# A graph network on one core: the first rows picked ahead of the rest, and the bias adds moved into layer 1's pairs

## The chip, the cores and the metric

The kernel runs on one core of a Trainium2 chip. The metric is the device time of one execution in microseconds. TensorE (PE in the profile, PEld for its weight loads), VectorE (DVE), ScalarE (ACT), GpSimd (POOL) and SyncE (SP) each work through a queue of their own in order and wait for each other by semaphores.

## The reference

Three edge-convolution layers over a graph of 2500 nodes and 80000 edges (sorted by `dst`), 256 features each. With h0 = relu(layernorm(x)):

```python
def _edge_conv(x, src, dst, W, b):
    xi = x[dst]
    xj = x[src]
    m = jnp.concatenate([xi, xj - xi], axis=-1) @ W + b
    s = jax.ops.segment_sum(m, dst, num_segments=N)
    cnt = jax.ops.segment_sum(jnp.ones((dst.shape[0],), m.dtype), dst, num_segments=N)
    return s / jnp.maximum(cnt, 1.0)[:, None]
...
for W, b in ((W0, b0), (W1, b1), (W2, b2)):
    h = jax.nn.relu(_edge_conv(h, src, dst, W, b))
    xs.append(h)
cat = jnp.concatenate(xs, axis=-1)
return cat @ Wf + bf
```

The result is x plus this. The message of an edge is linear in its two nodes, so a layer is h times (upper half of W minus lower half), plus the matrix A of edge counts between nodes times (h times the lower half), divided by the node's count of edges.

## The kernel before

The nodes are 20 tiles of 128 rows; `acc` holds one row of 256 numbers for each and gathers the result. The kernel has four parts.

**The head** (about the first 60 us) does three things at once, on all engines: it normalizes x and turns it (`hT`), it multiplies the tiles by the lower half of W0 (`pz`, split into a high and a low part, `zh` and `zl`) and by the first quarter of Wf, and it builds the first fifth of A. For A, the destinations are cut into windows of 6 nodes, 417 windows in four blocks of 128. To find where the edges of a window begin, `first` takes the first destination of each of 128 rows of `dst_i`; a product with a shifted identity on PE (`find_next`) puts the next row's first destination beside it; `find_rows` makes `behind` and `pick`, matrices of 128 x 512 (four blocks of 128 windows) which mark for every window the row that holds its limit; a product with `pick` fetches that row (`pick_half`, "pk"), ScalarE counts in it (`count_half`, "sg"), `search` ("se") works out a start, and POOL gathers 256 edges for every window (`get_edges`, "ge"). From the edges come keys, and from these, on DVE, `one_m` and `one_n` (`compare`, "B"), matrices of zeros and ones whose products on PE (`counts`, "C") are the counts of A.

The order of the head is written out by hand: `order` (L916) is a string of names with a number each, `perform` calls them one by one, and as nearly every engine call goes through `InOrder`, every engine's queue keeps that order. `st` are the statistics of two tiles, `rs`, `sq`, `sc` the steps to the scale and offset of a group of tiles, `N` their normalization (on DVE for tile 0, on ScalarE for tiles 1 to 3, on POOL from tile 4 on), `T` and `R` turning and taking what was turned, `Z` and `F` the products with W0 and Wf, `warm` a number of empty products of 128 x 512 put before the next product that asks for a bank of PSUM. "warm8" stands ahead of the product of `find_next`, "warm7" ahead of the first product with `pick`.

The x tiles come in five loads (`chunks`, L431). The third is on ScalarE's queue behind the load of `dst_i`, the others on SP's, where the loads of W0 and Wf stand between them. `small_numbers` ("io") turns three integer ramps into bfloat16 and float32.

**Layer 0** goes over five groups of destinations (504 columns, the last 486): PE multiplies zh and zl by the block of A (`a`), while the next block is built between the products and written to memory. In its last group, side work (`first_forms`) prepares layer 1: weights and the first two pairs of tiles are split into parts, and then four adds put the final bias `bf` on all 20 tiles of `acc`, 5 tiles (128 x 1280) each.

**Layers 1 and 2** begin with a node stage: for each of ten pairs of tiles (`Nodes`), DVE and ScalarE split `hT` (`Split`, into `staged`), PE multiplies by W and Wf (12 products), ScalarE and DVE take them into `zf`, `zh`, `zl`, `acc` and the sums `sh` and `sl`, and between these PE works off the last group of A alone (8 products for each pair of tiles). Then come the pairs: groups 0 and 1, then 2 and 3 of A, five chunks of four tiles each. A chunk takes seven products of combined blocks ("b11", "b21", "b22", "r1" to "r4") instead of eight. `Stream` (L1307) makes the blocks five steps ahead of PE: ScalarE copies b11, b21 and b22 into `block`; DVE adds in place for r1 and r2 (`staged` from `staged`), which ScalarE then copies; DVE writes r3 and r4 straight into `block`. The add of r2 writes over b22, so it waits until ScalarE has copied that.

**The end** multiplies layer 2's result by the last quarter of Wf and writes `acc` out.

Of the kernel before, what the change touches and what calls it, by code (L numbers as in the profile page):

```python
# [11 lines left out]
OP = mybir.AluOpType  # L12
# [301 lines left out]
def by_windows(ctx: ExitStack, tc: tile.TileContext, x, src, dst, Ws, bs, Wf, bf, out, missing):  # L314
    nc = tc.nc
    PE, DVE, ACT, POOL, SP = nc.tensor, nc.vector, nc.scalar, nc.gpsimd, nc.sync
    PEo, DVEo, POOLo, ACTo, SPo = (InOrder(tc, e) for e in (PE, DVE, POOL, ACT, SP))
    P = 128
    N, D = x.shape
    E = src.shape[0]  # L320
    NT = (N + P - 1) // P
# [5 lines left out]
    W = 6  # L327
    CH = 2
    S = 8
# [4 lines left out]
    WG = (NW + P - 1) // P  # L334
    IN_LAST = NW - (WG - 1) * P
    NB = NT * W
    N1 = NT * KEEP
# [52 lines left out]
    iota_m = const.tile([P, P], BF16, name="iota_m")  # L390
    iota_n = const.tile([P, NB], BF16, name="iota_n")
    deg = const.tile([P, WG, W], F32, name="deg")
    gsum = const.tile([P, WG, W + 2], F32, name="gsum")
    nc_ = const.tile([P, W + 2], F32, name="nc_")
    deg_b = const.tile([P, WG, W], BF16, name="deg_b")
    lim = const.tile([P, WG], F32, name="lim")
# [29 lines left out]
    def load_x(queue, a, b):  # L426
        queue.dma_start(acc[:, a:min(b, NT - 1), :], xr[:, a:min(b, NT - 1), :])
        if b == NT:
            queue.dma_start(acc[:LAST, NT - 1, :], x[(NT - 1) * P:N, :])

    chunks = [(0, 2), (2, 6), (6, 12), (12, 16), (16, NT)]  # L431
    load_x(SPo, *chunks[0])
    load_x(SPo, *chunks[1])
    load_x(ACTo, *chunks[2])
# [6 lines left out]
    def new_raw(l):  # L441
        raws[l] = raw_pools[-1].tile([P, DC, 2, D], F32, name="wbf", bufs=1)

    def load_wb(l, queue=SP):
        new_raw(l)
        ws[l] = (wts[l] if l == 1 else wpool.tile([P, DC, D], F32, name="wt")), raws[l][:, :, 0, :]
        queue.dma_start(ws[l][1], Ws[l][D:2 * D, :].rearrange("(c p) d -> p c d", p=P))
# [6 lines left out]
    def load_wf(l, queue=SP):  # L454
        if l == L:
            new_raw(l)
        wfs[l] = raws[l][:, :, 1, :]
        queue.dma_start(wfs[l], Wf[l * D:(l + 1) * D, :].rearrange("(c p) d -> p c d", p=P))

    load_wb(0, SPo)  # L460
    load_x(SPo, *chunks[3])
    load_wf(0, SPo)
    load_x(SPo, *chunks[4])
# [12 lines left out]
    im_i = pp.tile([P, NT * S], I32, name="im_i")  # L476
# [3 lines left out]
    nc_i = pp.tile([P, W + 2], I32, name="nc_i")  # L480
# [30 lines left out]
    limr = pp.tile([P, WG * P], F32, name="limr")  # L511
    first = pp.tile([P, 1], F32, name="first")
    after = pp.tile([P, 1], F32, name="after")
    behind = pp.tile([P, WG * P], F32, name="behind")
    pick = pp.tile([P, WG * P], F32R, name="pick")
# [8 lines left out]


    def small_numbers():
        DVEo.tensor_copy(iota_m, im_i[:, :P])
        DVEo.tensor_copy(iota_n.rearrange("p (c t) -> p t c", c=W), im_i.rearrange("p (t c) -> p t c", c=S)[:, :, 1:W + 1])
        DVEo.tensor_copy(nc_, nc_i)

    def limits():
        DVEo.tensor_copy(lim, lim_i)
# [16 lines left out]

    def find_rows():  # L550
        DVEo.tensor_add(after, ahead[0][:, 0:1], after)
        DVEo.tensor_scalar(behind, limr, after, None, op0=OP.is_gt)
        DVEo.scalar_tensor_tensor(pick, limr, first, behind, op0=OP.is_gt, op1=OP.subtract)

    row = pp.tile([P, WG], F32, name="row")

# [2 lines left out]
    def pick_half(i, o):  # L559
        pr = picked[i, o] = warmed(bank())  # L560
        PEo.matmul(pr[:, :HR], pick[:, i * P:(i + 1) * P], dst_r[:, o * HR:(o + 1) * HR], start=True, stop=True)

    def count_half(i, o):

        pr = picked.pop((i, o))
        junk = pp.tile([P, HR], BF16, name="junk1")
        ACTo.activation(junk, pr[:, :HR], AF.Sign, bias=unlim[:, i:i + 1], accum_out=base[:, o, i:i + 1])
        if o == 0:
            ACTo.copy(row[:, i:i + 1], pr[:, 0:1])
# [291 lines left out]
    def layer(l, g, a, own, PE=PE, ACT=ACT):  # L861
# [38 lines left out]
    a = new_a(0)  # L900
    acts = {
        "lim": limits, "first": find_first, "next": find_next, "pick": find_rows,
        "dstr": lambda: ACTo.copy(dst_r[:, MORE:], dst_i),
        "pk": lambda i: pick_half(i // 10, i % 10), "sg": lambda i: count_half(i // 10, i % 10),
        "se": lambda i: search(*((0, 1), (1, WG))[i]), "ge": get_edges,
        "aw": find_away, "ka": key_parts, "km": key_low, "kb": key_high, "kt": key_turn,
        "k1": lambda i: key_copy(i, 0), "k2": lambda i: key_copy(i, 1),
        "io": small_numbers, "ws": lambda: DVEo.tensor_sub(ws[0][0], ws[0][0], ws[0][1]),
        "st": stats, "rs": lambda g: spread(*groups[g]), "sq": lambda g: roots(*groups[g]),
        "sc": lambda g: scales(*groups[g]), "N": normalize, "T": turn, "R": take_turned,  # L910
# [3 lines left out]
        "warm": keep_warm,  # L914
    }
    order = """  # L916
        warm8 lim io first next dstr st0 rs0 sq0 pick sc0 warm7 N0 pk00 sg00 pk01 st1 T0 pk11 R0 sg01 st2 rs1 sq1 Z0 pk30 se0
        sg11 sc1 pk20 N1 st4 st5 sg30 ge0 T1 st6 R1 F0 sg20 pk21 st7 pk10 H0 F1 rs3 st3 sq3 sc3 G0 st9
        L0 sg21 N6 pk31 aw0 ka0 kb0 Z1 N5 st8 N7 G1 T6 rs4 sg10 sg31 km0 T5 se1 kt0 R6 H1 F6 sq4 sc4 k10 k20
        rs2 Z6 ge1 L1 T7 B0 R5 R7 Z5 B1 C0 B2 aw1 ka1 G6 H6 N9 H5 C1 T9 F7 E0 ge2 kb1 R9 sq2 km1 E1 kt1 C2 B3 k21 Z9  # L920
        k11 N8 L6 B4 sc2 aw2 E2 L5 C3 B5 C4 T8 E3 E4 C5 V9 ka2 ge3 kb2 R8 E5 H9 aw3 km2 Z7 N2 N3 C6 ka3 kb3 H7 F8 G7 B6 T2 R2
        km3 T3 E6 B7 L7 kt2 Z2 B8 B9 L9 C7 k22 k12 kt3 H2 N4 E7 B10 k13 k23 Z8 L2 C8 T4 C9 E8
# [40 lines left out]
    def flat(l):  # L963
        return raws[l].rearrange("p c t d -> p c (t d)") if l < L else wfs[l]
# [61 lines left out]
    def split_in_blocks(q, whole=True):  # L1026
        two = [block().rearrange("p c n -> p (c n)") for _ in range(2)]
        return Split(q, [two[0][:, :2 * D], two[0][:, 2 * D:], two[1][:, :2 * D]], whole)

    def first_forms():  # L1030
        DVEo.tensor_sub(ws[1][0], ws[1][0], ws[1][1])
        yield
        coming.append(Forms(flat(1), [flat(1)[:, c, :] for c in range(DC)]))
        coming[0].high()
        coming[0].low()
        yield
        coming[0].across()
        coming[0].last()
        yield
        for q in range(2):  # L1040
            split_in_blocks(q)
            yield
        for t in range(0, NT, 5):
            DVEo.tensor_add(acc[:, t:t + 5, :], acc[:, t:t + 5, :], bf_sb.unsqueeze(1).to_broadcast([P, 5, D]))
            yield

    extra = chain(degrees(0), finish(0, a), later_loads(), degrees(1))
    for g in range(NG):
        at = {}
        own = [NT] * 4 if g == 0 else [3, 3, 8, 8]  # L1050
        if g + 1 < NG:
            a1 = new_a(g + 1)
            one = build(g + 1, a1)
            left = -(-len([b for b in windows if b[0] == g + 1]) // TURN)
            units = NT + DC * DC
            at = {(i + 1) * (units - 4) // left - 1 for i in range(left)}
            if g:
                own = [sorted(at)[j] + 1 for j in ((5, 6, 9, 10) if g == 1 else (2, 3, 7, 8))]
        else:
            second.close()  # L1060
            raw_pools.append(ctx.enter_context(tc.tile_pool(name="raw", bufs=1, side="right")))
            bf_sb = raw_pools[-1].tile([P, D], F32, name="bf_sb")
            load_wb(1, SPo)
            load_wf(1, SPo)
            SPo.dma_start(bf_sb, bass.AP(tensor=bf.tensor, offset=bf.offset, ap=[[0, P], [1, D]]))
            ready = ctx.enter_context(tc.tile_pool(name="ready", bufs=7, side="right"))
            extra = chain(shares(), (None for _ in range(4)), first_forms())
# [34 lines left out]
    sl = late.tile([P, 2, Q * D + 32], F32R, name="sl")  # L1102
# [67 lines left out]
    class Pair:  # L1170
# [12 lines left out]
        def make(self, c, what, st, made):  # L1183
            to = made[what] = block()[:, :, :GS]
            b11, b21, b12, b22 = (st[:, g, h::2, :] for g in range(2) for h in range(2))
            if what[0] == "b":
                ACTo.copy(to, {"b11": b11, "b21": b21, "b22": b22}[what])
            elif what == "r1":
                DVEo.tensor_add(b12, b11, b12)
                ACTo.copy(to, b12)  # L1190
            elif what == "r2":
                DVEo.tensor_add(b22, b12, b22)
                ACTo.copy(to, b22)
            elif what == "r3":
                DVEo.tensor_sub(to, b11, b22)
            else:
                DVEo.tensor_add(to, b22, b21)
# [109 lines left out]
    class Stream:  # L1307
# [11 lines left out]
        def make(self, upto):  # L1319
            while self.n < min(upto, len(self.steps)):  # L1320
                m, p, c, part, what, made = self.steps[self.n]
                p.make(c, what, self.loaded[m], made)
                self.n += 1
                if self.n == len(self.steps) or self.steps[self.n][0] != m:
                    self.load(m + 4)
# [16 lines left out]
        tile_ = stage.tile([P, 4 * GS], F32R, name="staged")  # L1342
        Split(q, [tile_[:, k * 2 * D:(k + 1) * 2 * D] for k in range(3)])

    begun = []
    for l in range(1, L):
        order = orders[l]
        lone = Alone(l, order)
# [36 lines left out]
        after = orders[l + 1]  # L1385
# [27 lines left out]
    for i, q in enumerate(order):  # L1413
# [9 lines left out]
        for k in range(2):  # L1423
            t = 2 * q + k
# [58 lines left out]
```

## Time and profile before

| what | us |
|---|---|
| median of 3 runs | 471.52 (471.42 to 471.71) |
| the profiled execution's own time | 472.05 |
| its span in the profile | 470.2 |
| PE busy | 462.6 |
| DVE busy | 380.8 |
| ScalarE busy | 310.7 |
| POOL busy | 41.4 |

The span runs from the first to the last instruction of the kernel; the profiled execution's own time has 1.85 us more around it. All times in what follows are microseconds from the span's start. In a row of the timeline, the first number is the start, the second the length (of all instructions in the row, when there are several), and in brackets stands the idle time of that engine before the row with what ended it. Most instructions carry line 282, which is the helper that records them, so rows are told apart by the tiles that they write and read. Matmul ends are modelled, so PE's real rate is read from starts.

### The profile page before, as it was taken

Reading aid. Unit: us, or ns where it says so; the run is one execution under the profiler, and the core shown is the slowest. Engines: PE = TensorE matmul, PEld = TensorE weight load, DVE = VectorE, ACT = ScalarE, POOL = GpSimd, SP = SyncE. Lnnn points to the kernel's source line nnn. Section 1 sums busy time; section 2 is a strip of 40 time slices with the busy share of each in tenths; the row PEclk is TensorE's granted clock in tenths of the full one; section 3 lists DMA queues with packets and bytes.
Section 4 is the critical chain, followed back from the end, with each engine's and each line's share of the span. In section 5 each row is a group of like instructions: output and inputs, shape, how many; then the busy total and the mean of one; then the engine's idle time right before and its main releaser. Section 6 shows DMA issues by size and latency. Waiting matters only on the chain.

```text
span 470.2 us, 7370 instructions
## 1 busy us (share of the span) xinstructions
PE 462.6 (98%) x2739; PEld 365.7 (78%) x2739; DVE 380.8 (81%) x699; ACT 310.7 (66%) x543; POOL 41.4 (9%) x66
## 2 busy tenths in 40 slices
PE   8999999999999999999999999999999999999995
PEld 4888888787778878877887877877788788688685
DVE  8989898799898873499987847877899687578795
ACT  5777677685754441478769857785787798397540
POOL 3691015200101001000000000000000000000000
PEclk9999999999999999999999999999999999999998
DMA  8320084990824608531178551010212955220014
GB/s 277 93 55 3 1 165 78 193 215 13 178 44 84 139 0 166 113 118 59 46 237 313 177 176 55 36 45 1 88 44 89 352 177 199 88 89 0 1 62 160
DMA packets 21791, 52.07 MB, mean 111 GB/s; under 512 B 1959, under 2 KB 12150, under 8 KB 21750
## 3 DMA queue, kind: packets, MB, share of 16 engines
q1 hardware_dynamic: 14390, 33.41, 21.3%
q0 software_dynamic: 5856, 16.51, 18.3%
q10 hardware_dynamic: 1504, 1.63, 1.0%
q8 instruction: 22, 0.36, 0.3%
q14 instruction: 19, 0.16, 0.1%
HBM read 36.08 MB, written 15.46 MB: 110 GB/s over the span
## 4 chain that ended last, share of the span: by engine, by line
PE 89%; DVE 8%; DMA 1%; ACT 0%; issue 0%; DVEq 0%
PE bank L282 85%; PE pz L282 4%; DVE acc L282 2%; DVE st L282 1%; DVE one_m L282 1%; DMA acc<-in_x_dram 1%; DVE zl L282 1%; DVE one_n L282 1%; DVE staged L282 1%; DVE tmp L282 0%; DVE mv L282 0%; PE turned L282 0%; DVE kn L282 0%; DVE rs L282 0%; ACT junk L282 0%
## 5 line engine op out<-in xcount | busy, mean ns | idle before, releaser
L282 ACT CAST block<-staged 128x1008 fp32r<-128x1008 bf16 x120 | 117.9, 1031 | 16.7 <-DVE staged L282 6.4
L282 PE MATMUL bank<-block,zh 128*128 128x504 f32 (+1 forms) x200 | 83.7, 419 | 0.0
L282 PE MATMUL bank<-a,zh 128*128 128x504 f32 (+1 forms) x200 | 81.7, 408 | 0.0
L282 ACT CAST a<-bank 128x480 fp32r<-128x480 f32 (+1 forms) x105 | 54.4, 561 | 38.0 <-PE bank L282 36.2
L282 PE MATMUL bank<-a,zl 128*128 128x504 f32 (+1 forms) x200 | 77.8, 389 | 0.0
L282 PE MATMUL bank<-block,zl 128*128 128x504 f32 (+1 forms) x200 | 77.3, 387 | 0.0
L282 DVE TENSOR_TENSOR one_m<-iota_m,key_m 128x2048 bf16<-128x2048 bf16 (+2 forms) x55 | 64.4, 1171 | 9.9 <-PE bank L282 9.7
L282 PE MATMUL bank<-block,sh 128*128 128x504 f32 x160 | 68.9, 431 | 0.0
L282 PE MATMUL bank<-block,staged 128*128 128x512 f32 (+1 forms) x288 | 63.5, 370 | 0.3 <-DVE staged L282 0.2
L282 PE MATMUL bank<-block,sl 128*128 128x504 f32 x160 | 62.6, 391 | 0.0
L282 PEld LDWEIGHTS bank<-block,staged 128*128 128x128 f32 x288 | 49.2, 188 | 11.3 <-DVE staged L282 1.6
L282 DVE TENSOR_TENSOR block<-staged 128x1008 fp32r<-128x1008 bf16 x40 | 47.0, 1205 | 5.4 <-PE bank L282 4.1
L282 DVE TENSOR_TENSOR one_n<-iota_n,key_n 128x960 bf16<-128x960 bf16 (+2 forms) x110 | 51.3, 507 | 0.0
L282 PEld LDWEIGHTS <-one_m 128*128 128x128 bf16 x834 | 37.3, 97 | 13.9 <-issue 7.7
L282 PEld LDWEIGHTS bank<-block,zh 128*128 128x128 f32 x200 | 37.6, 188 | 10.8 <-issue 2.5
L282 PEld LDWEIGHTS bank<-block,zl 128*128 128x128 f32 x200 | 37.6, 188 | 10.6 <-issue 3.5
L282 PE MATMUL bank<-one_n,one_m 128*128 128x120 bf16 x834 | 44.7, 204 | 0.2
L282 PEld LDWEIGHTS bank<-a,zh 128*128 128x128 f32 x200 | 37.8, 189 | 6.4 <-issue 0.2
L282 PEld LDWEIGHTS bank<-a,zl 128*128 128x128 f32 x200 | 37.7, 189 | 6.3 <-issue 0.2
L282 DVE TENSOR_TENSOR staged<-staged 128x1008 bf16<-128x1008 bf16 x40 | 27.2, 679 | 17.4 <-ACT block L282 17.0
L282 PE MATMUL pz<-wbf,hT 128*128 128x256 f32 x160 | 38.8, 387 | 0.3 <-ACT hT L282 0.2
L282 PEld LDWEIGHTS bank<-block,sh 128*128 128x128 f32 x160 | 30.1, 188 | 10.4 <-issue 3.5
(163 smaller groups left out, 616.4 us busy)
## 6 DMA issues: line engine op xcount, KB each, us to landing
staged<-a_dram SPq DMA_DIRECT2D x52, 504.0 KB, 4.4
a_dram<-a POOLq DMA_DIRECT2D x20, 630.0 KB, 10.3
acc<-in_x_dram POOLq DMA_DIRECT2D x3, 640.0 KB, 11.9
out_dram<-acc SPq DMA_DIRECT2D x15, 128.0 KB, 1.7
acc<-in_x_dram SPq DMA_DIRECT2D x2, 512.0 KB, 8.9
wbf<-in_L_gnn_Wf_dram SPq DMA_DIRECT2D x4, 256.0 KB, 8.9
acc<-in_x_dram ACTq DMA_DIRECT2D x1, 768.0 KB
wbf<-in_L_gnn_W_dram SPq DMA_DIRECT2D x3, 256.0 KB, 6.1
```

What stands on the lines that cost most here:

```text
L282: return self.tc.keep_in_program_order(call(*args, **kwargs))
```

## The change

Two separate things.

In the head: `find_rows` marks rows for the first block of windows only; the other three blocks (384 columns) are marked by a new step "rest" of the order. The second load of x brings tiles 2 and 3 instead of 2 to 5, and tiles 4 and 5 come by a load of their own on SP's queue behind the lower half of W0. The three casts of `small_numbers` go from DVE to POOL. In the order, st0 stands ahead of `first`, "warm7" is "warm2", tiles 2 and 3 are normalized ahead of the search for block 0, the statistics of tiles 4 and 5 come after it, and three products with `pick` and one with W0 change places.

At layer 1: the four adds of `bf` leave `first_forms` and become a generator `add_bf`, which is advanced each time the blocks of an "r2" are made. It yields twice after each add, so the adds stand in DVE's queue ahead of the r2 of the first, third, fifth and seventh chunk of layer 1.

```diff
-    chunks = [(0, 2), (2, 6), (6, 12), (12, 16), (16, NT)]
+    chunks = [(0, 2), (2, 4), (6, 12), (12, 16), (16, NT)]
...
     load_wb(0, SPo)
+    load_x(SPo, 4, 6)
     load_x(SPo, *chunks[3])
...
     def small_numbers():
-        DVEo.tensor_copy(iota_m, im_i[:, :P])
-        DVEo.tensor_copy(iota_n.rearrange("p (c t) -> p t c", c=W), im_i.rearrange("p (t c) -> p t c", c=S)[:, :, 1:W + 1])
-        DVEo.tensor_copy(nc_, nc_i)
+        POOLo.tensor_copy(iota_m, im_i[:, :P])
+        POOLo.tensor_copy(iota_n.rearrange("p (c t) -> p t c", c=W), im_i.rearrange("p (t c) -> p t c", c=S)[:, :, 1:W + 1])
+        POOLo.tensor_copy(nc_, nc_i)
...
     def find_rows():
         DVEo.tensor_add(after, ahead[0][:, 0:1], after)
-        DVEo.tensor_scalar(behind, limr, after, None, op0=OP.is_gt)
-        DVEo.scalar_tensor_tensor(pick, limr, first, behind, op0=OP.is_gt, op1=OP.subtract)
+        rows_of(slice(0, P))
+
+    def rows_of(sl):
+        DVEo.tensor_scalar(behind[:, sl], limr[:, sl], after, None, op0=OP.is_gt)
+        DVEo.scalar_tensor_tensor(pick[:, sl], limr[:, sl], first, behind[:, sl], op0=OP.is_gt, op1=OP.subtract)
...
+        "rest": lambda: rows_of(slice(P, WG * P)),
...
-        warm8 lim io first next dstr st0 rs0 sq0 pick sc0 warm7 N0 pk00 sg00 pk01 st1 T0 pk11 R0 sg01 st2 rs1 sq1 Z0 pk30 se0
-        sg11 sc1 pk20 N1 st4 st5 sg30 ge0 T1 st6 R1 F0 sg20 pk21 st7 pk10 H0 F1 rs3 st3 sq3 sc3 G0 st9
-        L0 sg21 N6 pk31 aw0 ka0 kb0 Z1 N5 st8 N7 G1 T6 rs4 sg10 sg31 km0 T5 se1 kt0 R6 H1 F6 sq4 sc4 k10 k20
+        warm8 lim io st0 first next dstr rs0 sq0 pick sc0 warm2 N0 pk00 sg00 pk01 st1 rs1 T0 R0 rest sq1 sc1 sg01 Z0 pk11 N1 pk30 se0
+        sg11 st2 T1 sg30 pk20 st4 st5 ge0 R1 st6 F0 sg20 pk21 st7 pk10 H0 F1 rs3 st3 sq3 sc3 G0 st9
+        L0 sg21 N6 Z1 aw0 ka0 kb0 pk31 N5 st8 N7 G1 T6 rs4 sg10 sg31 km0 T5 se1 kt0 R6 H1 F6 sq4 sc4 k10 k20
...
+    def add_bf():
         for t in range(0, NT, 5):
             DVEo.tensor_add(acc[:, t:t + 5, :], acc[:, t:t + 5, :], bf_sb.unsqueeze(1).to_broadcast([P, 5, D]))
+            yield
             yield
...
                 m, p, c, part, what, made = self.steps[self.n]
+                if what == "r2":
+                    next(bias, None)
                 p.make(c, what, self.loaded[m], made)
...
-    begun = []
+    begun, bias = [], add_bf()
     for l in range(1, L):
```

## The prediction

> **What bounds the kernel now.** I read the page first: TensorE (PE) is busy nearly throughout, so a microsecond counts only where PE has to wait.
>
> ```profile
> span 470.2 us, 7370 instructions
> PE 462.6 (98%) x2739; PEld 365.7 (78%) x2739; DVE 380.8 (81%) x699; ACT 310.7 (66%) x543; POOL 41.4 (9%) x66
> ```
>
> Then the chain of waits in order of time (start, length, what). VectorE (DVE) carries it from the first x tiles to 32.41, then PE, except from 199.86 to 212.72.
>
> ```profile
> 0.74 4.16 DMA acc<-in_x_dram
> ...
> 6.18 0.50 DVE behind L282
> ...
> 6.71 0.75 DVE pick L282
> ...
> 31.51 0.90 DVE one_n L282 x2
> 32.41 0.04 issue
> 32.45 0.44 PE bank L282 x7
> ...
> 59.92 139.94 PE bank L282 x1186
> 199.86 0.04 DVEq L282
> 199.89 5.37 DVE acc L282 x4
> 205.26 0.61 DVE staged L282
> ...
> 212.72 252.64 PE bank L282 x1094
> ```
>
> So two stretches matter. In the timeline of the head, `first` waits for dst_i in time that DVE had free before x came, and PE's loads stop for DVE's one_n (0.32 us, and 0.21 more at 32.45):
>
> ```profile
> 4.71 0.15 DVE L282 CAST first<-dst_i 128x1 f32<-128x1 int32 x1 [0.56 <-DMA dst_i<-in_dst_dram]
> 5.12 0.56 PE L282 MATMUL bank<-first,shift 128*128 128x1 f32 x2
> 6.00 0.15 DVE L282 TENSOR_TENSOR after<-bank,after 128x1 f32<-128x1 f32 x1
> 32.13 0.11 PEld L282 LDWEIGHTS <-one_m 128*128 128x128 bf16 x2 [0.32 <-DVE one_n L282]
> ```
>
> From 14.4 to 32.4 the gaps of DVE's rows add to 0.31 us, nine of 0.034, each one instruction waiting for the one before it. Nothing there soaks up a delay.
>
> **Head, DVE.** In the built order st0 (two stats, two aggregates) stands ahead of `first`. Before, st0 runs from 4.92 and its last aggregate from 5.71 to 5.89; neighbours that don't depend overlap by 0.08, dependent ones stand 0.03 apart. So after: `first` 5.81 to 5.96, its memset 5.99 to 6.05. Before, 0.70 us lie between the memset's end (4.98) and the end of PE's shift product (5.68). `after` then starts at 6.05 + 0.70 + 0.03 = 6.78, not 6.00: +0.78.
> Next, behind and pick on 128 of 512. The 512-wide rows are 0.49 and 0.75, the narrowest of the same operations 0.15 and 0.16 (one or two elements); straight lines between give 0.24 and 0.31 for 128, 0.41 and 0.60 for 384. From `after` to the reciprocal it was 1.38 (6.00 to 7.38), now 0.18 + 0.26 + 0.23 = 0.67: -0.71. So the first block's pick ends at about 7.53 (7.46 before), and tile 0 is normalized at 7.83 (7.76): the first pick is no sooner.
> "rest" (384) comes back after the stats of tiles 2 and 3: 0.43 + 0.52 = +0.95. DVE's wait of 0.15 for ScalarE's count before 10.06 goes, since reciprocal and off now stand ahead of it: -0.15; rs waits for its own aggregate: +0.07. off of tiles 2 and 3 comes at 10.3 instead of 10.77, but the stats of tiles 8 and 9, which started at 10.85, start at 11.8. Sum +0.78 - 0.71 + 0.95 - 0.15 + 0.07 = +0.94. Bounds: PE's answer may have come only at 6.00, when `after` started (+0.32); if the split passes cost half of the estimate, about -0.35. So +0.6 to +1.3. I take +0.94: every row is close.
> All of it reaches the end: one_m and one_n stand behind it in the same queue, POOL's gathers and normalizations wait for start_i and off from it, and PE already waited for one_n at 32.13 and 32.45.
>
> **Head, the rest.** The three casts (0.21 + 0.42 + 0.29, started 3.60 to 3.86) leave DVE, which then waited for dst_i and x anyway: 0. On POOL they follow the cast of ident_b (0.47) that ends at 3.46; at 0.3 to 0.5 each they are done by 5, and POOL's next work is the gather at 10.97; their first reader on DVE is one_m at 21.50: 0. Its cover is that slack of 16 us.
> SP: one more issue (such rows are 0.45 to 0.50). Tiles 2 and 3 have fewer bytes ahead; DVE took them at 8.09 without a wait, so 0. Tiles 4 and 5 go behind W's lower half; no byte is added, and PE read that half at 9.61 without waiting for it, so they are there by about then; DVE now wants them at 10.9: 0, with 1.3 us to spare. Later loads are issued up to 1 us later: tiles 16 to 18 (issued 3.77, median 9.4 to landing) were read at 15.66, now at 16.6: 0. brow, read at 32.3, and wt, read at the end of the head, have longer still.
> PE: the seven empty products start from 5.55 to 7.38, while PE waits for pick (done at 7.46); with two it waits idle: 0, unless the clock follows (below). Tile 2's turn stopped 0.27 at 12.12 for ScalarE and comes sooner; PE only waits more at 32. One count and one pick product change places on ScalarE and PE; base waits for neither now.
>
> **Layer 1's start.** The four adds (1.48 each, 1.40 start to start, 5.6 in all) stand in front of the splits and the node work. The waits from 199 to 216:
>
> ```profile
> PEld bank L282 <- DVE staged L282: 1.6, 4, 0.5
> ```
>
> Layer 2 has the same 36 products without the adds: PE's starts go there from 331.05 to 340.04, 8.99 us; here from 205.15 to 214.93, 9.78. The difference is the stall: -0.79 (the three late starts, 0.21, 0.12 and 0.49 beyond the usual 0.23, add to 0.82). Without the adds the split can follow ScalarE's copy (ends 201.03) instead of starting at 205.18. Next to be late would be the following split: ScalarE's half starts at 206.38 and takes 0.63, two DVE passes 0.69 each, done at 208.5; PE wants it at 211.2. So the whole 0.79 goes; bounds 0.6 and 0.85.
> Among layer 1's pairs the adds stand ahead of "r2" in the first, third, fifth and seventh chunk, where DVE sat idle for ScalarE's copy of the same buffer:
>
> ```profile
> 251.14 0.69 DVE L282 TENSOR_TENSOR staged<-staged 128x1008 bf16<-128x1008 bf16 x1 [2.75 <-ACT block L282]
> 260.76 0.68 DVE L282 TENSOR_TENSOR staged<-staged 128x1008 bf16<-128x1008 bf16 x1 [1.10 <-ACT block L282]
> 272.79 0.68 DVE L282 TENSOR_TENSOR staged<-staged 128x1008 bf16<-128x1008 bf16 x1 [1.88 <-ACT block L282]
> 293.09 0.68 DVE L282 TENSOR_TENSOR staged<-staged 128x1008 bf16<-128x1008 bf16 x1 [1.17 <-ACT block L282]
> ```
>
> Four times 1.40 goes into 2.75, 1.10, 1.88 and 1.17: r2 is late by 0.30 and 0.23. Queued behind it are r3 and r4's blocks; in the third chunk r2's copy ended at 262.6 and PE reached that block near 266.0, 3.4 us later. Cost 0; if that cover were gone, +0.53.
>
> **Sum.** +0.94 - 0.79 = +0.15. The profiled execution took 472.05 (span 470.2 and 1.85 around it), so 472.2; it stands 0.53 over the median of the runs, so 471.52 + 0.15 = 471.7. A measurement tells about 0.2% (0.94 us) from no change: 470.58 to 472.46.
>
> **Rivals.** (1) Slower: PE's clock comes late. The empty products' loads start 0.43 us apart up to 6.36, then three follow in 0.53 from 6.74: the rate doubled near 6.7, 5.0 us after PE's first product, with PE fed all that while. After, PE has little between 5.2 and 9.65, where the first dense products start (9.61 before). If the 5.0 us count from there, PE runs at half rate to 14.65 and loses 2.5. PE has 0.32 + 0.21 + 0.94 = 1.47 to wait for DVE anyway, so 1.0 is left: 472.7. It decides once the half rate lasts beyond 12.6. For it: eight empties at full rate, up to 5.2, had not brought the clock. Against: PE isn't idle, with a shift product, two empties, two picks and four turns in those 4.4 us.
> [...]
> (2) Faster: PE, not DVE, sets the pace up to 32. Then tiles 2 and 3, 0.45 sooner, count and DVE's lateness doesn't: 471.52 - 0.45 - 0.79 = 470.3. For: PE has few gaps from 9.6 on. Against: its last stops there are for DVE's one_n.
> (3) PE's answer to `first` takes the 0.32 more and the adds' overshoot of 0.53 isn't covered: 471.67 + 0.85 = 472.5.
>
> **Numbers.** Forecast 0.52 (0.47 within 0.2%, 0.05 slower); clock 0.22 (0.19 slower, 0.03 within); faster rival 0.16 (0.11 faster, 0.05 within); (3) 0.10 (half slower). Faster 0.11, within 0.2% 0.60, slower 0.29. The range goes from just over (2) to a little above (1), 470.5 to 473.0; the forecast's own is 471.2 to 472.1.
>
> **What would show it.** `after` on DVE near 6.8 with idle time before it ended by PE; stats of tiles 8 and 9 near 11.8; PE's first a-product near 60.5 instead of 59.57; no PE wait for staged after layer 1's start; four adds in the idle stretches. I am wrong if `after` starts near 6.0, if the pz products from 9.6 stand 0.43 instead of 0.22 apart, or if blocks of the pairs arrive late.

## The result: slower by a quarter of a percent

| kernel | median of 11 runs each, same chip | lowest to highest |
|---|---|---|
| before | 471.71 | 471.42 to 472.06 |
| after | 473.09 | 472.07 to 473.42 |

The ratio is 1.0026, with a 95% interval of 1.0017 to 1.0035. So the change costs about 1.2 us. The forecast's own value was no measurable change (+0.15 us); what happened is its first rival, the late clock, with the sign that the prediction itself had named for being wrong: the pz products stand 0.43 apart. On the prediction's base of 471.52 the ratio makes 472.7, outside the forecast's own 471.2 to 472.1, but inside the whole range of 470.5 to 473.0; the median of 473.09 lies just above that range. That the range reaches so far is owed to the rival's price and not to the forecast. The profiled execution of after took 473.39, with a span of 471.6 (before: 472.05 and 470.2).

The page of before, its 40 slices of the granted clock (in tenths of full speed):

```profile
PEclk9999999999999999999999999999999999999998
```

The page of after, the same row and the shares of the chain by engine:

```profile
PEclk8899999999999999999999999999999999999999
...
PE 96%; ACT 1%; DMA 1%; DVE 1%; issue 0%; ACTq 0%
```

Before, VectorE (DVE) held a good part of the chain up to 32.41. Now PE holds nearly all of it: from 9.54 on the chain follows PE, with two stays on ScalarE, of about 1.5 us each, near 21 and 30. The timeline of PE in the head of before, the seven empty products and the first pz products:

```profile
5.55 2.22 PE L282 MATMUL bank<-idle 128*128 128x512 bf16 x7
...
9.61 1.96 PE L282 MATMUL pz<-wbf,hT 128*128 128x256 f32 x8 [0.23 <-ACT hT L282]
```

and of after:

```profile
6.17 0.35 PE L282 MATMUL bank<-first,shift 128*128 128x1 f32 x2 [0.94 <-DVE rs L282]
6.38 0.59 PE L282 MATMUL bank<-idle 128*128 128x512 bf16 x2
7.57 0.52 PE L282 MATMUL bank<-dst_r,pick 128*128 128x314 f32 x2 [0.60 <-DVE rs L282]
8.20 0.66 PE L282 MATMUL turned<-shift,acc 128*128 128x128 f32 x4
9.54 3.78 PE L282 MATMUL pz<-wbf,hT 128*128 128x256 f32 x8 [0.69 <-ACT hT L282]
```

Eight pz products take 3.78 us; before they took 1.96. Their starts are 0.43 apart until 15.63, then 0.22. The trace's records of the granted clock say when it changed: up at 5.49, down at 8.90, up again at 15.73. Before, there is one record in the head: up at 6.68, and the clock stays. The next view, stretches of after cut at those times, has as its columns the stretch, its length, and the busy time of PE, PE's loads, DVE, ScalarE and POOL; then the mean granted clock, the share of DMA and its GB/s:

```profile
2.08:5.49 3.41, 3.14 (x8) 0.86 (x6) 1.70 (x7) 1.87 (x3) 2.32 (x9) 1.00 0.93 307
5.49:8.90 3.41, 1.99 (x10) 1.06 (x10) 2.78 (x16) 1.36 (x6) 0.00 (x0) 1.00 1.10 358
8.90:12.31 3.41, 2.77 (x7) 2.23 (x8) 3.23 (x16) 2.28 (x6) 1.02 (x1) 0.50 1.10 349
12.31:15.73 3.42, 3.42 (x13) 2.97 (x12) 3.38 (x18) 2.02 (x7) 1.16 (x2) 0.50 0.70 209
```

and the same of before:

```profile
3.27:6.68 3.41, 3.41 (x10) 1.31 (x9) 2.72 (x17) 0.92 (x2) 0.19 (x1) 1.00 1.04 341
6.68:10.09 3.41, 3.00 (x14) 1.68 (x13) 3.22 (x14) 2.31 (x8) 0.00 (x0) 1.00 1.09 359
```

(The clock column says 1.00 before the first record too, although the first empties run at half rate, 0.43 apart. Only starts tell the rate there.) The first two records of after lie 3.41 us apart, so the stretches are cut to that length. In the one that ends at the first rise PE was busy 92% (3.14), in the one that ends at the fall 58% (1.99), then 81% (2.77) with no record at its end, and 100% (3.42) up to the second rise. In before it is 100% (3.41) up to the rise and 88% (3.00) behind it, and the clock stays. By what rule the clock changes the rows don't show.

DVE's part came as forecast. The timeline of DVE in before, the statistics of tiles 8 and 9:

```profile
10.85 0.75 DVE L282 BATCH_NORM_STATS2 st<-acc 128x6 f32<-128x256 f32 x2
```

The timeline of DVE in after:

```profile
6.56 0.16 DVE L282 TENSOR_TENSOR after<-bank,after 128x1 f32<-128x1 f32 x1 [0.44 <-PE bank L282]
6.75 0.29 DVE L282 TENSOR_SCALAR behind<-limr,after 128x128 f32<-128x128 f32 x1
7.08 0.35 DVE L282 SCALAR_TENSOR_TENSOR pick<-limr,first,behind 128x128 fp32r<-128x128 f32 x1
...
9.14 0.41 DVE L282 TENSOR_SCALAR behind<-limr,after 128x384 f32<-128x384 f32 x1
9.58 0.62 DVE L282 SCALAR_TENSOR_TENSOR pick<-limr,first,behind 128x384 fp32r<-128x384 f32 x1
...
11.78 0.72 DVE L282 BATCH_NORM_STATS2 st<-acc 128x6 f32<-128x256 f32 x2
```

The last row is again the statistics of tiles 8 and 9: 11.78, forecast 11.8. After that DVE itself waits for ScalarE (0.32 at 16.67, 0.34 at 21.77, 0.73 at 23.14), ScalarE for PE at half rate (2.08 for the pz products at 13.68), and from 9.54 to the first product with `a` no piece of the chain is DVE's.

Layer 1's start gains more than forecast. The waits there were 1.6 us on `staged` from DVE before; of after, the same view from 199 to 218:

```profile
PEld bank L282 <- DVE staged L282: 0.2, 1, 0.2
```

The four adds stand where the diff puts them, and nothing waits for them. The timeline of DVE in the pairs of after, two of the four places (the one with slack and the one without):

```profile
249.71 1.48 DVE L282 TENSOR_TENSOR acc<-acc,bf_sb 128x1280 f32<-128x1280 f32 x1
252.54 0.69 DVE L282 TENSOR_TENSOR staged<-staged 128x1008 bf16<-128x1008 bf16 x1 [1.35 <-ACT block L282]
...
260.97 1.48 DVE L282 TENSOR_TENSOR acc<-acc,bf_sb 128x1280 f32<-128x1280 f32 x1
262.37 0.68 DVE L282 TENSOR_TENSOR staged<-staged 128x1008 bf16<-128x1008 bf16 x1
```

The account of the two profiled executions: the first product with `a` moves from 59.57 to 61.99 (+2.42), layer 1's start gives 1.02 back, and from there to the end all products are 1.4 later, which is the difference of the spans. The table collects the milestones of all kernels below; "clock up" is the last time that the clock went up in the head, "against before" is median minus the median of the kernel before on the same chip (a single run in e10 to e12).

| kernel | clock up | first product with `a` | against before |
|---|---|---|---|
| before | 6.68 | 59.57 | |
| after | 15.73 | 61.99 | +1.38 |
| e1 bias adds alone | 7.59 | 59.66 | -1.13 |
| e2 head alone | 14.13 | 62.32 | +2.49 |
| e3 after, ten empties for eight | 5.40 | 60.53 | -0.32 |
| e4 before, two empties | 12.10 | 59.78 | +1.22 |
| e5 e1, two empties | 13.47 | 60.02 | +0.26 |
| e6 after, `first` ahead, seven empties | 6.16 | 59.56 | -0.67 |
| e7 after, seven empties | 5.66 | 60.40 | -0.20 |
| e8 e6, "rest" on GpSimd | 7.35 | 59.84 | -0.69 |
| e9 after, `first` ahead, two empties | 6.75 | 59.70 | -0.28 |
| e10 after again | 14.47 | 61.91 | +1.47 |
| e11 e4 again | 14.35 | 60.98 | +1.83 |
| e12 e5 again | 13.66 | 60.64 | +0.29 |

### The profile page after: what moved, and what is told of

It reads as the page before. It is cut to its first block, busy times and chain, and to the rows that moved or that the text cites. A ratio compares the mean times of both kernels' runs of the same rounds, so it can differ in the third digit from the quotient of the medians.

```text
span 471.6 us, 7368 instructions
## 1 busy us (share of the span) xinstructions
PE 462.4 (98%) x2734; PEld 367.2 (78%) x2734; DVE 381.0 (81%) x698; ACT 310.7 (66%) x543; POOL 41.7 (9%) x69
## 3 DMA queue, kind: packets, MB, share of 16 engines
q10 hardware_dynamic: 1504, 1.63, 1.0%
## 4 chain that ended last, share of the span: by engine, by line
PE 96%; ACT 1%; DMA 1%; DVE 1%; issue 0%; ACTq 0%
PE bank L282 88%; PE pz L282 8%; DMA acc<-in_x_dram 1%; PE turned L282 1%; ACT hT L282 0%; ACT junk L282 0%; DVE st L282 0%; ACT acc L282 0%; ACT km L282 0%; DVE acc L282 0%; ACT a L282 0%; DVE pick L282 0%; DVE behind L282 0%; DVE rs L282 0%; DVE mv L282 0%
## 5 line engine op out<-in xcount | busy, mean ns | idle before, releaser
L282 PE MATMUL pz<-wbf,hT 128*128 128x256 f32 x160 | 40.9, 403 | 0.8 <-ACT hT L282 0.7
L282 PEld LDWEIGHTS bank<-block,sl 128*128 128x128 f32 x160 | 30.1, 188 | 9.5 <-issue 3.7
```

Of the source, the lines that this page charges most:

```text
L282: return self.tc.keep_in_program_order(call(*args, **kwargs))
```

## The experiments

Theory B: the clock is late since PE is fed too thinly between the eight empties and the pz products, and that adds about 1.5 us to VectorE's lateness. Theory A is the prediction's sum, VectorE alone. From the fifth on, C is B with the blame on the five missing empties alone.

**e1, the bias adds alone.** The kernel before with `add_bf` and its calls:

```diff
+    def add_bf():
         for t in range(0, NT, 5):
             DVEo.tensor_add(acc[:, t:t + 5, :], acc[:, t:t + 5, :], bf_sb.unsqueeze(1).to_broadcast([P, 5, D]))
+            yield
             yield
...
+                if what == "r2":
+                    next(bias, None)
...
-    begun = []
+    begun, bias = [], add_bf()
```

> Only the second half of the change: the four bias adds move into layer 1's pairs, the head stays as before. Both theories expect the same: the stall at layer 1's start goes (-0.79 us, from 9.78 to 8.99 for the 36 products) and the adds are hidden in VectorE's idle time, so about 0.8 us less than before (0.9983 of it). If the adds cost something among the pairs, less than that is left.

Measured: 471.15 against 472.28, ratio 0.998 (0.997 to 0.9989). In the trace the head is 0.09 later and everything behind layer 1's start 0.93 earlier: the move gains 1.02. It beats both kernels, and nothing else that was run gained more against its own before (e6 and e8 lie within its interval).

**e2, the head alone.** After, with the adds back in `first_forms`:

```diff
-    def add_bf():
         for t in range(0, NT, 5):
             DVEo.tensor_add(acc[:, t:t + 5, :], acc[:, t:t + 5, :], bf_sb.unsqueeze(1).to_broadcast([P, 5, D]))
-            yield
             yield
...
-                if what == "r2":
-                    next(bias, None)
...
-    begun, bias = [], add_bf()
+    begun = []
```

> Only the first half: the new head, the bias adds where they were. Theory A (the forecast: VectorE's queue alone) expects +0.94 us, a ratio near 1.002, with PE's first a-product near 60.5. Theory B (VectorE plus a late TensorE clock) expects about +2.0 to +2.4 us (1.0042 to 1.0051) in executions whose clock doubles near 15 us, with the W0 products from 9.5 on 0.43 us apart, and a wide spread between executions.

Measured: 474.77 against 472.28, ratio 1.0052 (1.0039 to 1.0065). The head costs 2.5 us, not 0.94. Its trace has the clock up only at 14.13, with no earlier record.

**e3, PE fed ahead of the shift product.** After, with ten empties at the start instead of eight:

```diff
-        warm8 lim io st0 first next dstr rs0 sq0 pick sc0 warm2 N0 ...
+        warm10 lim io st0 first next dstr rs0 sq0 pick sc0 warm2 N0 ...
```

> The changed kernel with ten empty products instead of eight ahead of the product that follows `first`; nothing else. They fill TensorE's gap from 5.2 to 6.2. Theory B: the clock doubles before 9.5 again, the W0 products stand 0.22 apart, and what is left is VectorE's own lateness less the bias stall: +0.93 - 0.79, about 1.0003 of before, 1.2 us under the changed kernel. Theory A: no change against the changed kernel (1.0026 of before).

Measured: 471.96 against 472.28, ratio 0.9994 (0.9984 to 1.0005). Two more empty products take away most of the loss. Two stretches of 3.41 us of its trace, cut at its own record (up at 5.40):

```profile
1.99:5.40 3.41, 3.41 (x9) 1.21 (x8) 2.14 (x8) 1.84 (x3) 2.37 (x9) 1.00 1.00 312
5.40:8.81 3.41, 2.25 (x12) 1.06 (x10) 2.78 (x15) 1.31 (x5) 0.00 (x0) 1.00 1.09 360
```

Behind its record PE is busy 66% (2.25) and the clock stays up; in after it was 58% (1.99) and the clock fell. And with the clock in time, what is left is VectorE's lateness. Its chain of waits in time order:

```profile
31.36 1.13 DVE one_m L282
32.49 0.90 DVE one_n L282 x2
33.39 0.04 issue
33.43 0.44 PE bank L282 x7
```

`one_n` is 0.98 later than before (31.51), PE's product behind it 0.98 (32.45), the first product with `a` 0.96. The prediction's sum for DVE was 0.94.

**e4, the missing empties alone.** Before, with two empties for seven:

```diff
-        warm8 lim io first next dstr st0 rs0 sq0 pick sc0 warm7 N0 ...
+        warm8 lim io first next dstr st0 rs0 sq0 pick sc0 warm2 N0 ...
```

> The kernel before with two empty products instead of seven ahead of the first product with pick; nothing else. If the five missing empty products are what makes the clock late, the W0 products from 9.6 on stand 0.43 apart here too and the time grows by 1 to 2.5 us. If it is the gap that the later `first` opens ahead of the product of find_next, TensorE is fed to 6.4 here, the clock doubles near 6.7 and the time is that of before (0 to +0.2 us).

Measured: 473.5 against 472.28, ratio 1.0024 (1.0013 to 1.0034), single runs from 472.39 to 474.37. So the empties alone can make the clock late. The stretches of its trace between its records (up at 5.28, down at 8.69, up at 12.10) and the one ahead of them:

```profile
1.87:5.28 3.41, 3.41 (x9) 1.07 (x7) 2.78 (x13) 1.91 (x3) 1.58 (x8) 1.00 0.95 289
5.28:8.69 3.41, 1.70 (x10) 0.96 (x10) 3.23 (x13) 1.29 (x5) 0.00 (x0) 1.00 1.09 357
8.69:12.10 3.41, 3.33 (x9) 2.24 (x8) 3.12 (x19) 3.01 (x11) 1.03 (x1) 0.50 1.10 348
```

But in this execution the head is only 0.21 late at the first product with `a`; 1.4 more goes at layer 1's start. There ScalarE waits for the load of a quarter of Wf, then come its forms, two splits and the four adds:

```profile
193.46 1.06 ACT L282 ACTIVATE block<-wbf 128x1024 fp32r<-128x1024 f32 x1 [9.50 <-DMA wbf<-in_L_gnn_Wf_dram]
```

That is 14.1 us after the load's issue (12.7 before, 12.7 to 13.0 in e1 to e3 and after). Two causes lie in one execution; e5, e11 and e12 take them apart.

**e5, the missing empties without the adds in the way.** e1 with two empties for seven (the diff of e4).

> The kernel before with the bias adds moved (which measured 471.15) and two empty products for seven; nothing else of the head. Theory C, the clock alone: the five empty products that are missing let TensorE's clock come late in many executions, at a different time in each, and cost 0.8 to 1.2 us on average: 472.0 to 472.4. Rival D: the trace of the kernel before with two empties shows its first a-product only 0.21 later, and 1.4 more lost at layer 1, where the load of Wf landed 14.1 instead of 12.7 us after its issue and the bias adds stood behind it; that is chance, or something that the moved adds are immune to. Then this kernel stays at 471.2 to 471.5.

Measured: 472.02 against 471.76, ratio 1.0009 (1.0 to 1.0017); e1's was 0.998. The empties cost 1.4 us by these two ratios; e5's single runs go from 471.14 to 473.16. In its trace the clock goes up at 6.64, down at 10.05 behind 3.41 us in which PE was busy 64% (2.18), and up at 13.47. The head is 0.45 late, 0.36 against e1, and Wf's quarter came late again, 15.1 us after its issue, which costs 0.77 at layer 1's start even without the adds there. The size fits C, the trace splits it as D does: not settled by this run.

**e6, `first` ahead of st0, PE fed.** After with two changes in the order:

```diff
-        warm8 lim io st0 first next dstr rs0 sq0 pick sc0 warm2 N0 ...
+        warm8 lim io first next dstr st0 rs0 sq0 pick sc0 warm7 N0 ...
```

> The changed kernel with first and the shift product ahead of st0 again, and seven empties as before; the split of find_rows, the loads, the casts and the rest of the order stay changed. Theory C with VectorE's sum of the prediction (+0.78 for first behind st0, -0.71 +0.95 -0.15 +0.07 for the rest): the clock comes early, the head is +0.16 against before and layer 1 -1.02: 0.86 under the kernel before, near 471.4; its first a-product near 59.7. Rival: the +0.96 that the fed kernel showed comes from the split and the new order and not from first's place: then it stays at 471.9 to 472.0, first a-product near 60.5.

Measured: 471.09 against 471.76, ratio 0.9984 (0.9975 to 0.9993), first product with `a` at 59.56. Its DVE has no wait for PE there:

```profile
5.66 0.17 DVE L282 TENSOR_SCALAR rs<-mv 128x2 f32<-128x2 f32 x1
5.73 0.15 DVE L282 TENSOR_TENSOR after<-bank,after 128x1 f32<-128x1 f32 x1
```

So the split of find_rows, the other loads and the rest of the order cost nothing (-0.01 where +0.16 was worked out; `dst_i` came 0.3 earlier in this execution), and VectorE's 0.96 in e3 is nearly all `first` behind st0. The cleanest pair for this is e7 below, which differs from e6 only in that place: its first product with `a` comes at 60.40, 0.84 later. As a whole it is no quicker than e1: the new head brings nothing by itself.

**e7, the seven empties alone put back.** After, with the order's warm2 as warm7.

> The changed kernel with seven empties instead of two behind the shift product, so that only the idle 0.9 us ahead of the shift product is left of what PE's feed lost. If the missing empties are what makes the clock late, it comes early and the time is near that of the fed kernel, 471.9 to 472.3. If the idle stretch ahead of the shift product is enough, the empties run at half rate, 7 x 0.43 from 6.4 to 9.4, the first product with pick starts at 9.4 instead of 7.57 and the time is 473 to 474.5.

Measured: 471.56 against 471.76 by medians, ratio 1.0007 (0.9996 to 1.0017). The runs fall into two groups: seven from 471.40 to 471.64, four from 472.84 to 473.43. The trace is of the first group, with the clock up at 5.66; the row of its seven empties takes 1.67 (2.22 in before), and in the 3.41 us behind the record PE is busy 79% (2.69):

```profile
2.25:5.66 3.41, 2.97 (x7) 0.76 (x5) 2.26 (x8) 1.70 (x3) 2.12 (x8) 1.00 0.94 329
5.66:9.07 3.41, 2.69 (x15) 1.63 (x15) 2.74 (x16) 1.57 (x6) 0.00 (x0) 1.00 1.09 359
```

Neither of the two expectations holds for every run. That the slower group is the one with the late clock is inferred from the size of the gap, 1.2 us and more; no trace of that group was kept.

**e8, "rest" on GpSimd.** e6 with the other three blocks' rows marked by GpSimd:

```diff
+    def rest_of_rows():
+        sl = slice(P, WG * P)
+        POOLo.tensor_scalar(behind[:, sl], limr[:, sl], after, None, op0=OP.is_gt)
+        POOLo.tensor_scalar(reach, limr[:, sl], first, None, op0=OP.is_gt)
+        POOLo.tensor_sub(pick[:, sl], reach, behind[:, sl])
...
-        "rest": lambda: rows_of(slice(P, WG * P)),
+        "rest": rest_of_rows,
```

> As the kernel with first ahead and seven empties, but the other three blocks' rows are marked on GpSimd (two compares and a subtraction of 128 x 384), which had no work between 4.4 and 10.97; VectorE loses the 0.95 us of rest. If VectorE sets the head's pace: stats of tiles 8 and 9 near 10.1, the head 0.79 sooner than before at one_n, and as TensorE waited 0.53 for one_n, 0.4 to 0.6 of it reaches the first a-product (near 59.1); with layer 1's -1.02 the time is 1.4 to 1.6 under the kernel before, 470.7 to 470.9. If TensorE or the gathers set the pace, it stays at the time of the kernel with rest on VectorE, or at 471.15, that of the bias adds moved alone.

Measured: 471.07 against 471.76, ratio 0.9986 (0.9977 to 0.9995), the same as e6: the 0.4 to 0.6 did not come. The timeline of its DVE shows why:

```profile
6.33 0.55 DVE L282 SCALAR_TENSOR_TENSOR pick<-limr,first,behind 128x128 fp32r<-128x128 f32 x1
...
9.49 0.17 DVE L282 RECIPROCAL rs<-rs 128x2 f32<-128x2 f32 x1 [0.76 <-ACT rs L282]
```

the timeline of its ScalarE:

```profile
8.19 0.52 ACT L282 ACTIVATE junk<-bank,unlim 128x314 bf16<-128x314 f32 x1 [0.40 <-PE bank L282]
```

and the timeline of its POOL:

```profile
6.08 1.34 POOL L282 TENSOR_SCALAR behind<-limr,after 128x384 f32<-128x384 f32 x1 [1.73 <-DVE after L282]
7.42 1.29 POOL L282 TENSOR_SCALAR reach<-limr,first 128x384 f32<-128x384 f32 x1
8.79 1.00 POOL L282 TENSOR_TENSOR pick<-reach,behind 128x384 fp32r<-128x384 f32 x1
```

DVE only waits sooner, 0.76 us for ScalarE's root, which stands behind the first count of block 0 and the first turned tiles there. That count had itself waited 0.40 for PE's first product with `pick`, at 7.66 (7.03 in e6): in this execution the clock went up only at 7.35 and the seven empties ahead of it took 2.63 (2.08 in e6). And the pick of 128 that runs beside GpSimd's compare took 0.55 instead of 0.35; why is not tried.

**e9, the idle stretch alone taken away.** After, with `first next dstr` ahead of `st0` and the two empties kept.

> The changed kernel with first and the shift product ahead of st0 again, but its two empties kept: the idle 0.9 us ahead of the shift product is gone, the five empties stay missing. If the five empties decide (theory C), the clock is late in many executions and the time is 0.8 to 1.5 above that of the same kernel with seven empties, which was 0.16% under the kernel before: the same as the kernel before or up to 0.15% above it, with single runs spread over 2 us. If the idle stretch ahead of the shift product decides, it is like the kernel with seven, 0.16% under.

Measured: 471.36 against 471.64, ratio 0.9998 (0.9988 to 1.0007). Again two groups: eight runs from 470.74 to 471.60, three from 472.35 to 472.53. The trace is of the first; its 3.41 us on either side of the record (up at 6.75):

```profile
3.34:6.75 3.41, 3.05 (x9) 0.98 (x7) 2.43 (x15) 0.92 (x2) 1.03 (x4) 1.00 1.04 362
6.75:10.16 3.41, 2.54 (x12) 1.94 (x13) 3.17 (x16) 2.73 (x9) 0.00 (x0) 1.00 1.09 355
```

So in this head C's blame on the empties alone is wrong: with five of them missing, but the shift product in its old place, most executions have the clock in time, by their times. Either repair, e7's or e9's, brings back most executions; after has both faults at once. In the old head it is otherwise: e4 and e5 have the shift product in its old place too, and their clock is late in all four traces (e11 and e12 are the second of each). One difference that the rows show is the wait of PE for `pick`, which has 512 columns there and 128 here. The timeline of PE in e4:

```profile
7.62 0.52 PE L282 MATMUL bank<-dst_r,pick 128*128 128x314 f32 x2 [1.60 <-DVE rs L282]
```

and in e9:

```profile
6.83 0.53 PE L282 MATMUL bank<-dst_r,pick 128*128 128x314 f32 x2 [0.45 <-DVE rs L282]
```

In e5, e11 and e12 that wait is 1.03 to 1.07. So what the empties are worth may depend on the waits that they fill; no run tries this by itself.

**e10, the changed kernel again,** unchanged, profiled once more, for the time at which its pz products go over from 0.43 to 0.22 apart (15.63 in the first profile).

> The changed kernel itself, one more look. [...] If the clock counts from the program's own products, it is 15.7 again within 0.3.

Measured: 473.11. The clock goes up once, at 14.47, against 15.73 in the first profile of the same program, though the shift product stands at 6.02 for 6.17 and the eight empties at 1.63 in both: the program alone doesn't fix that time. Here there is no earlier record: the row of the two empties takes 1.01 (0.59 in the first profile), eight pz products from 10.06 take 3.78. Stretches of 3.41 us counted back from its record:

```profile
4.23:7.64 3.41, 2.44 (x8) 0.68 (x6) 2.08 (x12) 0.92 (x2) 0.14 (x2) 1.00 1.05 355
7.64:11.05 3.41, 2.72 (x8) 2.01 (x9) 3.13 (x14) 2.79 (x9) 0.00 (x0) 1.00 1.10 353
11.05:14.47 3.42, 3.42 (x11) 2.82 (x10) 3.38 (x16) 0.88 (x3) 2.17 (x2) 1.00 0.95 287
```

At the end of the first two, with PE busy 72% (2.44) and 80% (2.72), no record stands; at the end of the third, with 100% (3.42), the clock goes up. The first product with `a` is at 61.91, within 0.1 of the first profile, since what the clock gained at 14.47 the picks and turns lost before 10.06.

**e11, e4 again, and e12, e5 again,** both unchanged, for the load of Wf.

> The kernel before with two empties for seven, one more look: where the clock doubles (12.3 in the first look), and how long after its issue the load of the quarter of Wf lands (14.1 in the first look, 12.7 to 13.0 in the kernels with the clock in time). If that landing is chance, it is 12.6 to 13.1 now, the head is 0.2 to 2 late by the clock and layer 1 as in the kernel before. If it goes with this kernel, it is 14 or more again.

> The kernel with the bias adds moved and two empties for seven, one more look, for the same two things: the clock doubled near 13.0 and the load of Wf landed 15.0 after its issue in the first look. Chance: 12.6 to 13.1 now, and the clock at another time. Tied to this kernel: 14 or more again.

Measured: 473.47 and 471.93. The first product with `a` is 1.41 and 0.98 later than in before and in e1, with the clock up at 14.35 and 13.66, and the load is read 12.7 us after its issue in both. The row of e11 that answers to e4's:

```profile
193.24 1.06 ACT L282 ACTIVATE block<-wbf 128x1024 fp32r<-128x1024 f32 x1 [8.08 <-DMA wbf<-in_L_gnn_Wf_dram]
```

So the late load doesn't come with these kernels every time, and the clock alone can cost 1.0 to 1.4 here. What made the load late in e4 and e5 stays open.

## Why the prediction was wrong where it was

**The empties.** The step that failed is "with two it waits idle: 0, unless the clock follows". The clock followed. The condition was named, and as a rival it got a chance of 0.22 with this against it: "PE isn't idle, with a shift product, two empties, two picks and four turns in those 4.4 us". What the runs showed in its place: not idle, but busy only 58% (after), 50% (e4) and 64% (e5) of the 3.41 us at whose end the clock fell. The trace of before had the material for counting PE's waits: the row of the seven empties is 2.22 long and runs to 7.77, where two end near 6.4 (their row is 0.59 in e4, 1.01 in e5) and PE then waits for pick until 7.5; and `first` behind st0 opens an idle 0.94 ahead of the shift product.

**The rival's price** was 1.0, with the clock up at 14.65. It went up at 15.73: from 9.54 that is 6.19 us at half rate, 3.1 lost; 0.53 of waiting for `one_n` and VectorE's 0.96 lie beside it, so 1.6 should be left. Measured: 2.42 - 0.96 = 1.46. The form of the sum was right and its main term 0.6 too small (2.5 for 3.1): it counted 5.0 us from the first dense product, where the record of after stands 6.19 behind it. That the 5.0 us of before count again from the first dense product was the author's estimate, and no run shows it. That the rival's 472.7 meets the ratio's 472.7 is in part luck, as the gain at layer 1 was forecast 0.23 too small and the two errors offset each other.

**The clock's records** stand at another time in each execution: the first rise at 6.68 in before, 5.49 in after, 14.47 in e10 with the same program as after. No single wait of PE tells the cases apart: between the first empties and the pz products its longest were 0.94, 0.60 and 0.69 in after and 1.60 in e4, and the clock fell in both; in e7 0.92 and 0.69, and it stayed up. The forecast's sum lies 1.0 below the ratio's 472.7.

**DVE's sum**, +0.94, held: +0.96 in e3, +0.83 in e7, where the clock is in time. That it is so close is in part luck, since its terms moved against each other: `after` at 6.56, not 6.78 (PE answered 0.5 us after the memset, not 0.7); behind and pick on 128 took 0.29 and 0.35 for 0.24 and 0.31. In after itself the term reaches nothing: PE, at half rate, is later. The first rival had that right.

**Layer 1's start**, forecast -0.79, is -1.02 in e1, e3 and after alike. The mechanism was right, the span was cut one product short: 214.93 is the start of the last of the 36 products and 340.04 that of the product behind them. With 215.16 it is 10.01 against 8.99. The three late starts that seemed to confirm it (0.82) were three of five; the other two are 0.11 and 0.10 late. The bound of 0.85 was therefore too low.

**The hidden parts** were hidden: POOL's casts run at 3.45, 3.68 and 3.98 and the next work there is the gather; tiles 4 and 5 are taken at 10.90 without a wait; r2 of the third chunk follows its add without idle time and PE doesn't stop for it.

**The other rivals.** That PE sets the pace and gains (2) was half true: PE sets it, at half rate, and nothing is gained. Rival (3)'s two terms, a late answer of PE and uncovered adds, didn't occur.

**The sum again:** 0.96 that DVE's lateness costs by itself (e3), 1.46 that the clock adds to it, -1.02 for the adds: +1.4, against +1.38 by medians. The 1.46 is what is left of the 2.42 and not measured apart.

## What to carry to other kernels

Work that is there only to keep PE busy can be worth time to everything behind it: five empties fewer cost 1.2 us in e4 and 1.4 in e5. When such work is taken out, or a gap is opened beside it, look in the trace at the records of the granted clock and at the starts of the products behind them (0.22 or 0.43 apart here). One profile shows one execution; e10 shows another record for the same program (14.47 for 15.73), and groups in the times of single runs (e7, e9) hint at more.

When an instruction waits for a load and is cheap itself, as `first` here, its place in the queue is worth what waits for it on other engines (0.84 us between e6 and e7), not its own 0.15 us.

When comparing a stretch in two layers, count both from and to the start of the same product.

## What was not expected

The clock can go up and be lost again in the head: up at 5.49, down at 8.90 (after); 5.28 and 8.69 (e4); 6.64 and 10.05 (e5). PE's busy share of the 3.41 us beforehand doesn't settle it by itself: 87% in e7 (2.97) stood ahead of a rise, while 87% in e11 (2.98 from 7.52) and in e12 (2.98 from 3.42) had no record at the end. Ahead of the three falls it was 50% (e4), 58% (after) and 64% (e5); behind a rise after which the clock stayed up it was 66% in e3, 74% in e9 and 79% in e7. Row ends are modelled, and no run varies this share alone: how the clock is decided is not shown.

The load of a quarter of Wf is read 12.7 to 13.0 us after its issue in before, after, e1 to e3, e7, e8, e11 and e12, and after 14.1 and 15.1 in e4 and e5. With the four adds in front of layer 1 such an execution lost 1.4 us there (e4), without them 0.77 (e5): moving the adds also takes away part of this exposure.
